# A transformer kernel of four blocks: the order of the first loads, the queue of the residual rows, the room of the returning probabilities and the place of a weight product

## The chip, the cores and the metric

The kernel runs on one core of a Trainium2 chip. The metric is the device time of one execution in microseconds (us), as the median of several runs. A core has five engines, each with its own instruction stream: TensorE (PE: matrix products and transposes through the array; PEld is its weight load), VectorE (DVE), ScalarE (ACT), GpSimd (POOL) and SyncE (SP). In this kernel nearly all DMA transfers are issued by SP, some by POOL. An engine works through its own stream in order: an instruction that waits holds everything behind it on the same engine, DMA issues included.

## The reference

x has the shape (2, 1024, 512): 2048 tokens, 16 tiles of 128. Four blocks with residuals; the second and the fourth are the same FFN:

```python
x = x + attn_a(layernorm(x), ...)   # chunked linear attention with decay
x = x + ffn(layernorm(x), ...)      # quantised codes: (w - 128) * scale
x = x + attn_b(layernorm(x), ...)   # softmax attention
x = x + ffn(layernorm(x), ...)      # the same weights again
```

```python
# attn_a, per chunk of 128 tokens and head of 128 (4 heads)
k     = k / max(norm(k), 1e-12)
cla   = cumsum(log(sigmoid(x Wa + ba) + 1e-6))
attn  = (q k^T) * beta * tril(exp(cla - cla^T))
y     = attn v + (q state) * exp(cla)
state = state * exp(cla_end) + v^T (k * beta * exp(cla_end - cla))
# ffn, hidden 1408
out = qlinear(silu(qlinear(x, gate)) * qlinear(x, up), down)
# attn_b, one head of 512, no mask
out = softmax(Q K^T / sqrt(512)) V Wo
```

Everything is float32.

## The kernel before

**Precision.** [...] `split` (L68) writes the high half with ScalarE and the difference with VectorE (or with GpSimd where `eng` says so). `mm3` (L82 to L87) then makes a product from three: high x high (L83), high x low (L84), low x high (L85). A product of 128x128 weights with 512 columns is one instruction of the "128x512" kind. `load_split` (L73) loads a block of 128x512 into a staging room (`stg`, four rooms) and splits it. `parts` collects the low halves' instructions, so that later code can be placed behind them.

**Order.** The program is traced, and a scheduler then sets the order of the instructions of each engine from its own estimate of times. `behind(list)` (L61) forces what is issued inside it to come after the instructions in the list; it is used as an order, not as a semaphore. Memory is given out by pools: a tile with a tag takes one of the tag's rooms and waits until the room's last reader is done.

**The opening** (L655 to L693). Warming matmuls, then M = Wq Wk^T (`weight_product`, L149; it is computed because attention B needs it; names pM, operands "M"), in four blocks over the inner dimension: each block is one lhs and one rhs of 128x512. Between the blocks come the layer norms of the first four token tiles (`ln_tile`, `layernorm_T`, L113): statistics on VectorE (L102, L104), the inverse root on GpSimd (`rs`, L108), the normalised tile `xn` (L110), four transposes in the array (`pxT`, L118), and the split of the result (`xh`, `xl`). Then the projections with Wk (pWk), Wq (pq) and Wv (pWv), for which each weight block is loaded and split. `spill` (L166) splits M and stores it to DRAM (`m_d`).

**Attention A** (loop L714 to L752) goes over the 16 token tiles. One iteration has the projections of a later tile, the scores (pS), the decay, the local part (pl, L640), the state's part (pg, L645), the state's update (pd, L606), and work of the next stages (`fill[t]`, `moving`). Decay needs a row of cumulated logs that returns through DRAM (`load_row`, row, L512 on GpSimd and L532 on SP). For the norm of k, ss (L572, L573, VectorE) gives s by a power on GpSimd (L575), and s times beta (L576) is used in `at` (L625), which pl reads. kw (L583, GpSimd) is what pd reads. In the last three iterations the second weight product, V = Wv Wo (pV, four blocks, `product_operands`, L140, used by attention B), and the first products of the FFN stand between the tiles. In the last-but-one iteration the order is: decay(15), then fill, down_weights, V's blocks 1 and 2, the last k norm (`late_norm`, behind those blocks' splits), the FFN's first weights, and three `moving` steps (`combine`, L229: differences `xT_f` of token halves and their splits B_f and T_f).

**FFN** (`ffn`, used twice as f and g): seven products of half matrices per hidden block (pX, pY, pZ, pV with weights wcf or wcg, L324), then the down projection (pof, pog, L870 and L871). Its gate and up weights are combined by GpSimd once (`stationary`, L297, lines L307 to L310), stored in DRAM and loaded back for later passes (L313).

**Attention B.** Scores of two 128-row tiles at a time stand in four PSUM banks (psX, psY, psZ, psV, L969). `softmax` (L1004): maximum on VectorE (L1007, L1009), exponential on ScalarE into a room tagged `pe` (L1014), sum and its inverse. `probs_T` (L1022) must turn the tile of probabilities so that the array can use it as weights: VectorE turns blocks of 32x32 (`py`, L1041), SP stores this to DRAM (`p_d`, L1045), and four loads bring it back in its new order (L1056). These land in the room of `ptl`, the low half, and are split there in place by `probs_split` (L1061: `pth` high, `ptl` low). Tile 14 alone is turned by TensorE (`ppt`, L1036). Tile 15 alone lands in a room tagged `pe` ("raw"). `out_b` (L1073) loads the residual rows (`xrb`, L1077), multiplies the probabilities with v (pob, 24 products per tile), adds (L1081) and stores the rows to x3 (L1082). The tags `pe`, `py`, `ptl`, `pth` have two rooms each; `xres`, where xrb stands, has three, so the load of tile t's rows waits until the rows of tile t-3 are stored. All of L1045, L1056, L1077 and L1082 are on SP's queue, in the scheduler's order.

**GpSimd in the span of attention B**: the inverse roots for the norms (`rs_b`, `rs_g`, L108) and some moves of turned tokens (`ln_move`, L188, DMA issue L196: `xT_b`, `xT_g`). Nothing of `xrb`.

Of the kernel before, what the change touches and what calls it, by code (L numbers as in the profile page):

```python
# [9 lines left out]
F32 = mybir.dt.float32  # L10
# [6 lines left out]
P = 128  # L17
D = 512
KD = D // P
T = 1024  # L20
NB = 2
NT = NB * T // P
# [3 lines left out]
ST = 4  # L26
# [8 lines left out]
def hybrid_block_kernel(ctx: ExitStack, tc: tile.TileContext, a, out):  # L35
# [34 lines left out]
        c = nc.scalar.copy(hi, src)  # L70
        return c.ins, (eng or nc.vector).tensor_tensor(lo, src, hi.bitcast(F32), ALU.subtract).ins  # L71

    def load_split(w, sp, src_ap, name, eng=None):  # L73

        stg = sp.tile([P, 512], F32, tag="stg", name=f"stg_{name}")
        load = nc.sync.dma_start(out=stg, in_=src_ap).ins
        cast, low = split(w[:, 0:512], w[:, 512:1024], stg, eng)
        parts.append(low)
        return cast, load
# [33 lines left out]
    def layernorm_T(xin, xT, i, name):  # L113

        xn = layernorm(xin, name)
        ps = psum(f"pxT_{name}").rearrange("p (k c) -> p k c", k=KD)
        for k in range(KD):
            nc.tensor.transpose(ps[:, k, :], xn[:, k * P : (k + 1) * P], ident)  # L118
        xh, xl = xT
        cs = bass.ts(i, P)  # L120
        split(xh[:, :, cs], xl[:, :, cs], ps)

    cols = cp.tile([P, H + 2 * KH], F32, name="cols")
    bq_s, sg_s, su_s = cols[:, 0:H], cols[:, H : H + KH], cols[:, H + KH : H + 2 * KH]
# [12 lines left out]
    m_d = [dp.tile([P, 1024], F32, tag=f"m_{k}", name=f"m_{k}") for k in range(KD)]  # L137


    def product_operands(sp, lhsT_d, rhs_d, name, k):  # L140

        w = slot(f"{name}{k}")
        lw, rw = w[:, 0:1024], w[:, 1024:2048]
        load_split(lw, sp, lhsT_d[k * P : (k + 1) * P, :], f"{name}l{k}")
        eng = nc.gpsimd if name == "M" else None
        cast, _ = load_split(rw, sp, rhs_d[k * P : (k + 1) * P, :], f"{name}r{k}", eng)
        return lw, rw, cast

    def weight_product(operands, name):  # L149
# [184 lines left out]
    with ExitStack() as actx:  # L334
# [41 lines left out]

        def load_wqkv(nm, staged=None):
            two = [slot(f"{nm}{n}") for n in range(2)]
            wqkv[nm] = [two[k // 2][:, k % 2 * 1024 : (k % 2 + 1) * 1024] for k in range(KD)]
            for k in range(KD):  # L380
                w, eng = wqkv[nm][k], nc.gpsimd if k % 2 else None
                if staged is None:
                    _, load = load_split(w, sp, a[nm][k * P : (k + 1) * P, :], f"{nm}{k}", eng)
                else:
                    split(w[:, 0:512], w[:, 512:1024], staged[:, k], eng)
            return load if staged is None else None

        xa = [x_in[t * P : (t + 1) * P, :] for t in range(NT)]

        def ln_tile(t):  # L390
            st, i = divmod(t, ST)
            if i == 0:
                xTa[st] = new_xT(f"a{st}")
            tag = "xres" if t < 8 and t % 4 > 1 else "xin"
            layernorm_T(xs[t] if t < 4 else load_x(xa[t], f"a{t}", tag), xTa[st], i, f"a{t}")

        def gate_proj(st):

# [258 lines left out]
            nc.tensor.matmul(pw[:, 0:P], ones, ones, start=i == 0, stop=i == WARM - 1)  # L657
        loads, xs = [], []
        prep = weight_product(loads, "M")
        loads.append(product_operands(sp, a["WqT"], a["WkT"], "M", 0))  # L660
        for k in range(KD):
            if k + 1 < KD:
                loads.append(product_operands(sp, a["WqT"], a["WkT"], "M", k + 1))
            if k < 2:
                xs += [load_x(xa[t], f"a{t}", "xres" if t > 1 else "xin") for t in (2 * k, 2 * k + 1)]
            if k == 2:

                staged = yp.tile([P, 4, KD, ST, 32], F32, tag="y", name="y_Wk")
                staged = staged.rearrange("p k a b c -> p k (a b c)")
                for m in range(KD):  # L670
                    nc.sync.dma_start(out=staged[:, m], in_=a["Wk"][m * P : (m + 1) * P, :])
                load_wab()
            pm, end = next(prep)
            with behind((end, loads[-1][2])):
                for t in ((), (0, 1), (2, 3), ())[k]:
                    ln_tile(t)
        load_consts()
        with behind((*normed_x, *parts[-2:])):
            load_wqkv("Wk", staged)
        with behind((end,)):  # L680
            kv_part(0, "Wk")
        wq_loaded = load_wqkv("Wq")
        spill(ap, ("kT", "kw", "sdec", "at"), pm, m_d, "M")
        for i in range(4):
            ends.clear()
            q_head(0, i)
# [27 lines left out]
        for t in range(NT):  # L714
            if t + 4 < NT:
                q_head(*divmod(t + 4, ST))
            if t == 0:
                decay_rows(0)
                load_row(0)
                load_row(1)  # L720
            load_row(t + 1)
            if (t + 2) % ST:
                load_row(t + 2)
            if t + 1 < NT:
                kv_tile(t + 1)
            weighed = scores(t)
            if t + 1 < NT:
                with behind((*normed[t + 1][2:], *key_copy)):
                    decay(t + 1)
            with behind(normed.get(t + 1, (weighed,))):  # L730
                for step in fill[t]:
                    step()
                if 1 <= t <= KH:
                    down_weights(sp, t - 1)
                for n in {NT - 3: (0,), NT - 2: (1, 2), NT - 1: (3,)}.get(t, ()):
                    loads.append(product_operands(sp, a["WvT"], a["Wo"], "V", n))
                if t == NT - 2:
# [161 lines left out]
    with ExitStack() as bctx:  # L899
# [122 lines left out]
        def probs_T(b, i):  # L1022


            t = b * NK + i
            pe, ri = pes[t]
            if t == NT - 2:

                lo = bp.tile([P, NK, P], F32R, tag="ptl", name=f"ptl{t}")
                hi = bp.tile([P, NK, P], F32R, tag="pth", name=f"pth{t}")  # L1030
                for s in range(2):
                    ps = psum(f"ppt{t}_{s}").rearrange("p (k c) -> p k c", k=4)
                    ks = slice(s * 4, s * 4 + 4)
# [11 lines left out]
            nc.sync.dma_start(  # L1045
                out=p_d[i].rearrange("k p f -> p k f"), in_=y.rearrange("p (k f) -> p k f", k=NK)
            )
            lo = bp.tile([P, NK, P], F32R, tag="ptl", name=f"ptl{t}")
            hi = bp.tile([P, NK, P], F32R, tag="pth", name=f"pth{t}")
            raw = lo.bitcast(F32)  # L1050
            if t == NT - 1:

                raw = bp.tile([P, T], F32, tag="pe", name=f"raw{t}").rearrange("p (k c) -> p k c", k=NK)
            placed = p_d[i].rearrange("k (c j) (r q) -> r j (k c) q", c=4, r=4)
            for r in range(4):
                nc.sync.dma_start(  # L1056
                    out=raw[32 * r : 32 * (r + 1)].rearrange("p k (c q) -> p (k c) q", c=4), in_=placed[r]
                )
            ptT[t] = hi, lo, raw, ri
# [13 lines left out]
        def out_b(b, i):  # L1073
            t = b * NK + i
            hi, lo, _, ri = ptT[t]
            xr = rp.tile([P, D], F32, tag="xres", name=f"xrb{t}")
            nc.sync.dma_start(out=xr, in_=x2[t])  # L1077
# [4 lines left out]
            nc.sync.dma_start(out=x3[t], in_=xr)  # L1082
            return end
# [189 lines left out]
```

## Time and profile before

| | us |
|---|---|
| median of 3 runs | 950.49 (950.21 to 950.91) |
| the profiled execution | 951.1 |
| its span in the trace | 949.4 |
| TensorE busy | 935.0 |
| VectorE busy | 725.2 |
| ScalarE busy | 412.0 |
| GpSimd busy | 219.1 |
| mean granted TensorE clock | 0.996 |

The profile is of one execution. A line of the timeline gives the start, the duration, the engine, the source line, the operation, what is written and what is read (by the program's names, buffer numbers left out), and in brackets how long the engine stood idle before it and what released it. "PE pl L640 <- DVE at L625: 2.2, 1, 2.2" in the list of waits says that the product pl waited for VectorE's `at`, 2.2 us in total, once, 2.2 us at the longest. In the windows, the number before "(x..)" is an engine's busy time in that stretch; then come the mean granted clock of TensorE, the DMA engines' share and GB/s.

By the chain of work that ended last, 86% of the span belongs to TensorE, 5% to VectorE and 3% to DMA:

```profile
PE 86%; DVE 5%; DMA 3%; SPq 2%; ACT 2%; issue 1%; POOL 1%; ACTq 0%; POOLq 0%; DVEq 0%
```

### The profile page before, as it was taken

The page shows a single profiled execution, that of the slowest core. Times are in us where ns is not written, and L with a number is a line of the kernel's source. Part 1 is how long each engine was busy: PE and PEld are TensorE (multiplying, and loading weights), DVE is VectorE, ACT ScalarE, POOL GpSimd, SP SyncE. Part 2 cuts the span into 40 slices and gives each one's busy share as a digit, 9 for nine tenths or more (in the row PEclk, how much of TensorE's full clock was granted, in tenths as well). Part 3 has the DMA queues.
Part 4 walks back from the last instruction along what each step waited for, and adds up shares of the span by engine and source line. Part 5 has one row for each costly group of instructions (what it writes and reads, how often), then busy time and mean ns, then how long its engine had stood idle before and what let it go on. Part 6 is the DMA issues. An engine that isn't in the chain of part 4 may idle for free.

```text
span 949.4 us, 13214 instructions
## 1 busy us (share of the span) xinstructions
PE 935.0 (98%) x4402; PEld 775.8 (82%) x4402; DVE 725.2 (76%) x1457; ACT 412.0 (43%) x795; POOL 219.1 (23%) x318
## 2 busy tenths in 40 slices
PE   8999999999999999999999999999989999999998
PEld 7788888887788888888888888888878888888887
DVE  7757767778899699787947877658868876976655
ACT  6554434336466434454324534235434443534421
POOL 5333323443355011120120400030400431001100
PEclk9999999999999999999999999999999999999999
DMA  9526456674898458742761989326989762573022
GB/s 322 178 90 175 137 133 167 186 193 161 292 363 267 106 199 298 183 84 78 264 146 45 173 167 212 135 36 132 190 166 312 276 169 45 189 243 137 37 65 81
DMA packets 215861, 162.18 MB, mean 171 GB/s; under 512 B 150960, under 2 KB 166640, under 8 KB 215792
## 3 DMA queue, kind: packets, MB, share of 16 engines
q1 hardware_dynamic: 213488, 156.61, 56.6%
q0 software_dynamic: 2304, 4.72, 3.3%
q8 instruction: 35, 0.57, 0.3%
q14 instruction: 34, 0.28, 0.1%
HBM read 104.76 MB, written 41.84 MB: 154 GB/s over the span
## 4 chain that ended last, share of the span: by engine, by line
PE 86%; DVE 5%; DMA 3%; SPq 2%; ACT 2%; issue 1%; POOL 1%; ACTq 0%; POOLq 0%; DVEq 0%
PE pXf L324 4%; PE pog L871 4%; PE pog L870 4%; PE pZf L324 4%; PE pVg L324 4%; PE pVf L324 4%; PE pZg L324 4%; PE pXg L324 4%; PE pof L871 3%; PE pof L870 3%; PE pob L85 3%; PE pob L83 3%; PE pob L84 3%; PE psV L969 2%; PE psZ L969 2%; PE psX L969 2%
## 5 line engine op out<-in xcount | busy, mean ns | idle before, releaser
L870 PE MATMUL pog<-wdg,hsg 128*128 128x512 f32 (+1 forms) x165 | 60.1, 375 | 0.0
L871 PE MATMUL pog<-wdg,hsg 128*128 128x512 f32 (+1 forms) x165 | 60.1, 375 | 0.0
L871 PE MATMUL pof<-wdf,hsf 128*128 128x512 f32 x154 | 59.3, 390 | 0.4 <-DVE ve_b L106 0.4
L870 PE MATMUL pof<-wdf,hsf 128*128 128x512 f32 x154 | 59.2, 390 | 0.0
L83 PE MATMUL pob<-vh,pth 128*128 128x512 f32 x128 | 50.8, 397 | 2.5 <-ACT pth L70 2.5
L85 PE MATMUL pob<-vh,ptl 128*128 128x512 f32 x128 | 50.8, 397 | 0.0
L84 PE MATMUL pob<-vl,pth 128*128 128x512 f32 x128 | 50.4, 394 | 0.0
L71 POOL TENSOR_TENSOR hsg<-sgg,hsg 128x128 fp32r<-128x128 f32 x40 | 17.9, 469 | 130.9 <-ACT hsg L70 130.9
L324 PE MATMUL pVf<-T_f,wcf 128*128 128x512 f32 x176 | 46.6, 389 | 0.0
L324 PE MATMUL pXg<-B_g,wcg 128*128 128x512 f32 x176 | 46.6, 389 | 0.0
L324 PE MATMUL pXf<-B_f,wcf 128*128 128x512 f32 x176 | 46.5, 394 | 0.0
L324 PE MATMUL pVg<-T_g,wcg 128*128 128x512 f32 x176 | 46.3, 389 | 0.0
L108 POOL TENSOR_TENSOR rs_b<-ve_b,mhalf 128x1 f32<-128x1 f32 x16 | 11.6, 728 | 141.6 <-DVE ve_b L106 137.4
L108 POOL TENSOR_TENSOR rs_g<-ve_g,mhalf 128x1 f32<-128x1 f32 x16 | 9.6, 604 | 137.9 <-DVE ve_g L106 137.9
L196 POOL DMA_DIRECT2D xT_g<-y_g x48 | 30.9, 652 | 40.5 <-DVE T_b L71 29.0
L324 PEld LDWEIGHTS pXf<-B_f,wcf 128*128 128x128 f32 x176 | 33.3, 190 | 7.1 <-DMA wcf<-wc 0.3
L324 PEld LDWEIGHTS pVf<-T_f,wcf 128*128 128x128 f32 x176 | 33.1, 188 | 6.9
L324 PEld LDWEIGHTS pVg<-T_g,wcg 128*128 128x128 f32 x176 | 33.1, 188 | 6.9
L324 PEld LDWEIGHTS pXg<-B_g,wcg 128*128 128x128 f32 x176 | 33.0, 188 | 6.9
L870 PEld LDWEIGHTS pog<-wdg,hsg 128*128 128x128 f32 x165 | 31.1, 188 | 5.7
L871 PEld LDWEIGHTS pog<-wdg,hsg 128*128 128x128 f32 x165 | 31.0, 188 | 5.6
L871 PEld LDWEIGHTS pof<-wdf,hsf 128*128 128x128 f32 x154 | 28.9, 188 | 6.8 <-DVE hsf L71 0.8
(335 smaller groups left out, 2737.9 us busy)
## 6 DMA issues: line engine op xcount, KB each, us to landing
wcg<-wc SPq DMA_DIRECT2D x22, 896.0 KB, 5.8
wc<-wcf SPq DMA_DIRECT2D x11, 896.0 KB, 5.3
wcf<-wc SPq DMA_DIRECT2D x11, 896.0 KB, 5.6
p<-py SPq DMA_DIRECT2D x15, 512.0 KB, 4.0
ptl<-p SPq DMA_DIRECT2D x56, 128.0 KB, 4.0
xin_a<-in_x SPq DMA_DIRECT2D x16, 256.0 KB, 4.5
xra<-in_x SPq DMA_DIRECT2D x16, 256.0 KB, 2.7
row<-cl SPq DMA_DIRECT2D x16, 256.0 KB, 3.7
```

Source lines behind the costliest of these rows:

```text
L71: return c.ins, (eng or nc.vector).tensor_tensor(lo, src, hi.bitcast(F32), ALU.subtract).ins
L83: nc.tensor.matmul(ps, lhs_hi, rhs_hi, start=first, stop=False)
L84: nc.tensor.matmul(ps, lhs_hi, rhs_lo, start=False, stop=False)
L85: end = nc.tensor.matmul(ps, lhs_lo, rhs_hi, start=False, stop=last).ins
L108: nc.gpsimd.tensor_tensor(rs, ve, mhalf, ALU.pow)
L196: (nc.sync if sync else nc.gpsimd).dma_start(out=xf[32 * b : 32 * (b + 1), :, c, :], in_=y[32 * c : 32 * (c + 1), b].rearrange("p k i q -> ...
L324: nc.tensor.matmul(ps, w[:, m, k * P : (k + 1) * P], o[:, s, k, :], start=first and k == 0 and s == 0, stop=k == 1 and s == 1, skip_group_ ...
L870: nc.tensor.matmul(ps, hs[i][0][:, j], wd[j][:, ds], start=j == 0, stop=False)
L871: nc.tensor.matmul(ps, hs[i][1][:, j], wd[j][:, ds], start=False, stop=j == KH - 1)
L969: ends[nm] = nc.tensor.matmul(ps, o[:, i, k], w[:, j, k], start=first and k == 0 and i + j == 0, stop=k == 1 and i == 1, skip_group_check= ...
```

## The change

1. **Opening loads.** All eight blocks of M are loaded first. The blocks 2 and 3 go to a room tagged `y` that is free at that time, instead of waiting for `stg` rooms. Then come the four token tiles, Wab, Wk (now in the `stg` rooms), the constants, and Wq (now staged in the `y` room). pM's blocks are ordered among the token tiles: tiles 0 and 1 behind block 2, tiles 2 and 3 behind block 3. M's spill is placed behind Wq's splits. `layernorm_T` returns its last transpose for this.
2. **Rows of the decay.** `load_row(t + 2)` is written at the end of an iteration instead of its beginning. `decay(t + 1)` for the tiles 7 and 15, which have no `normed[t + 1][2:]`, is placed behind that of the tile before.
3. **V.** V's blocks 1 and 2, and the k norm of the last tile, are issued before the rest of the last-but-one iteration, behind `key_copy` alone.
4. **Probabilities.** The four loads of every tile (not of tile 15 alone) land in a room tagged `pe`, which the exponentials use too. The split reads it there and writes `pth` and `ptl`.
5. **Residual rows.** xrb's 16 loads are issued by GpSimd's queue instead of SP's.

In the order that is built, the engines' streams differ so: in the opening TensorE runs blocks 0 to 2 of pM, the transposes of tiles 0 and 1, block 3, the transposes of tiles 2 and 3, pWk, and so on; GpSimd makes M's low halves 2 and 3 before the first `rs_a`. At V, VectorE's splits of blocks 1 and 2 stand before xT_f's first difference, `ss` and s x beta of tile 15 directly behind V's splits, and `at` of tile 15 before two T_f splits; GpSimd's s of tile 15 stands behind four of the weight sums instead of six; row 15 stands behind kw of tile 14. In attention B, ScalarE's `pth` casts of tiles 3, 5 and 7 stand before or nearer to the exponentials of later tiles, and 16 products of FFN g stand after the second of the 24 products of pob15. The xrb loads stand between `rs_b`, `rs_g` and the xT_g moves on GpSimd.

```diff
-    def load_split(w, sp, src_ap, name, eng=None):
-
-        stg = sp.tile([P, 512], F32, tag="stg", name=f"stg_{name}")
+    def load_split(w, sp, src_ap, name, eng=None, stg=None):
+
+        if stg is None:
+            stg = sp.tile([P, 512], F32, tag="stg", name=f"stg_{name}")
...
-    def product_operands(sp, lhsT_d, rhs_d, name, k):
+    def product_operands(sp, lhsT_d, rhs_d, name, k, rooms=(None, None)):
...
-        load_split(lw, sp, lhsT_d[k * P : (k + 1) * P, :], f"{name}l{k}")
+        load_split(lw, sp, lhsT_d[k * P : (k + 1) * P, :], f"{name}l{k}", None, rooms[0])
...
-        loads.append(product_operands(sp, a["WqT"], a["WkT"], "M", 0))
+        room = staging("M")
         for k in range(KD):
-            if k + 1 < KD:
-                loads.append(product_operands(sp, a["WqT"], a["WkT"], "M", k + 1))
-            if k < 2:
-                xs += [load_x(xa[t], f"a{t}", "xres" if t > 1 else "xin") for t in (2 * k, 2 * k + 1)]
...
-            pm, end = next(prep)
-            with behind((end, loads[-1][2])):
-                for t in ((), (0, 1), (2, 3), ())[k]:
-                    ln_tile(t)
+            rooms = (room[:, 2 * k - 4], room[:, 2 * k - 3]) if k > 1 else (None, None)
+            loads.append(product_operands(sp, a["WqT"], a["WkT"], "M", k, rooms))
+        xs += [load_x(xa[t], f"a{t}", "xres" if t > 1 else "xin") for t in range(ST)]
+        load_wab()
+        split_M = parts[-2:]
+        turned = []
+        for k in range(KD):
+            with behind(turned):
+                pm, end = next(prep)
+            with behind((end,)):
+                turned = [ln_tile(t) for t in ((), (), (0, 1), (2, 3))[k]]
+        with behind((*normed_x, *split_M)):
+            load_wqkv("Wk")
         load_consts()
-        with behind((*normed_x, *parts[-2:])):
-            load_wqkv("Wk", staged)
+        staged = staging("Wq")
+        for m in range(KD):
+            wq_loaded = nc.sync.dma_start(out=staged[:, m], in_=a["Wq"][m * P : (m + 1) * P, :]).ins
         with behind((end,)):
             kv_part(0, "Wk")
-        wq_loaded = load_wqkv("Wq")
-        spill(ap, ("kT", "kw", "sdec", "at"), pm, m_d, "M")
+        with behind(load_wqkv("Wq", staged)):
+            spill(ap, ("kT", "kw", "sdec", "at"), pm, m_d, "M")
...
-            if (t + 2) % ST:
-                load_row(t + 2)
...
-                with behind((*normed[t + 1][2:], *key_copy)):
+                with behind((*(normed[t + 1][2:] or normed[t][2:]), *key_copy)):
                     decay(t + 1)
+            if t == NT - 2:
+                with behind(key_copy):
+                    for n in (1, 2):
+                        loads.append(product_operands(sp, a["WvT"], a["Wo"], "V", n))
+                with behind(parts[-4:]):
+                    late_norm.pop()()
...
-                for n in {NT - 3: (0,), NT - 2: (1, 2), NT - 1: (3,)}.get(t, ()):
+                for n in {NT - 3: (0,), NT - 1: (3,)}.get(t, ()):
                     loads.append(product_operands(sp, a["WvT"], a["Wo"], "V", n))
-                if t == NT - 2:
-                    with behind(parts[-4:]):
-                        late_norm.pop()()
...
+            if (t + 2) % ST:
+                load_row(t + 2)
...
-            raw = lo.bitcast(F32)
-            if t == NT - 1:
-
-                raw = bp.tile([P, T], F32, tag="pe", name=f"raw{t}").rearrange("p (k c) -> p k c", k=NK)
+
+            raw = bp.tile([P, T], F32, tag="pe", name=f"raw{t}").rearrange("p (k c) -> p k c", k=NK)
...
-            nc.sync.dma_start(out=xr, in_=x2[t])
+            nc.gpsimd.dma_start(out=xr, in_=x2[t])
```

More of the change, by code (lines that the diff above doesn't have):

```diff
@@ L117, in layernorm_T @@
         for k in range(KD):
-            nc.tensor.transpose(ps[:, k, :], xn[:, k * P : (k + 1) * P], ident)
+            turned = nc.tensor.transpose(ps[:, k, :], xn[:, k * P : (k + 1) * P], ident).ins
         xh, xl = xT
@@ L121, in layernorm_T @@
         split(xh[:, :, cs], xl[:, :, cs], ps)
+        return turned
     cols = cp.tile([P, H + 2 * KH], F32, name="cols")
@@ L137, in hybrid_block_kernel @@
     m_d = [dp.tile([P, 1024], F32, tag=f"m_{k}", name=f"m_{k}") for k in range(KD)]
-    def product_operands(sp, lhsT_d, rhs_d, name, k):
+    def product_operands(sp, lhsT_d, rhs_d, name, k, rooms=(None, None)):
         w = slot(f"{name}{k}")
         lw, rw = w[:, 0:1024], w[:, 1024:2048]
-        load_split(lw, sp, lhsT_d[k * P : (k + 1) * P, :], f"{name}l{k}")
+        load_split(lw, sp, lhsT_d[k * P : (k + 1) * P, :], f"{name}l{k}", None, rooms[0])
         eng = nc.gpsimd if name == "M" else None
-        cast, _ = load_split(rw, sp, rhs_d[k * P : (k + 1) * P, :], f"{name}r{k}", eng)
+        cast, _ = load_split(rw, sp, rhs_d[k * P : (k + 1) * P, :], f"{name}r{k}", eng, rooms[1])
         return lw, rw, cast
@@ L378, in load_wqkv @@
             two = [slot(f"{nm}{n}") for n in range(2)]
+            done = []
             wqkv[nm] = [two[k // 2][:, k % 2 * 1024 : (k % 2 + 1) * 1024] for k in range(KD)]
@@ L384, in load_wqkv @@
                 else:
-                    split(w[:, 0:512], w[:, 512:1024], staged[:, k], eng)
-            return load if staged is None else None
+                    done.extend(split(w[:, 0:512], w[:, 512:1024], staged[:, k], eng))
+            return load if staged is None else done
         xa = [x_in[t * P : (t + 1) * P, :] for t in range(NT)]
@@ L394, in ln_tile @@
             tag = "xres" if t < 8 and t % 4 > 1 else "xin"
-            layernorm_T(xs[t] if t < 4 else load_x(xa[t], f"a{t}", tag), xTa[st], i, f"a{t}")
+            return layernorm_T(xs[t] if t < 4 else load_x(xa[t], f"a{t}", tag), xTa[st], i, f"a{t}")
         def gate_proj(st):
@@ L659, in hybrid_block_kernel, with staging @@
         prep = weight_product(loads, "M")
-        loads.append(product_operands(sp, a["WqT"], a["WkT"], "M", 0))
+        def staging(name):
+            y = yp.tile([P, 4, KD, ST, 32], F32, tag="y", name=f"y_{name}")
+            return y.rearrange("p k a b c -> p k (a b c)")
+        room = staging("M")
         for k in range(KD):
-            if k + 1 < KD:
-                loads.append(product_operands(sp, a["WqT"], a["WkT"], "M", k + 1))
-            if k < 2:
-                xs += [load_x(xa[t], f"a{t}", "xres" if t > 1 else "xin") for t in (2 * k, 2 * k + 1)]
[L666 to L672, printed above, removed]
-            pm, end = next(prep)
-            with behind((end, loads[-1][2])):
-                for t in ((), (0, 1), (2, 3), ())[k]:
-                    ln_tile(t)
+            rooms = (room[:, 2 * k - 4], room[:, 2 * k - 3]) if k > 1 else (None, None)
[11 more added lines that the diff above has]
+            load_wqkv("Wk")
         load_consts()
-        with behind((*normed_x, *parts[-2:])):
-            load_wqkv("Wk", staged)
+        staged = staging("Wq")
+        for m in range(KD):
+            wq_loaded = nc.sync.dma_start(out=staged[:, m], in_=a["Wq"][m * P : (m + 1) * P, :]).ins
         with behind((end,)):
             kv_part(0, "Wk")
-        wq_loaded = load_wqkv("Wq")
-        spill(ap, ("kT", "kw", "sdec", "at"), pm, m_d, "M")
+        with behind(load_wqkv("Wq", staged)):
+            spill(ap, ("kT", "kw", "sdec", "at"), pm, m_d, "M")
         for i in range(4):
```

## The prediction

> **What bounds the kernel now.** I read the totals first, then TensorE's list of waits, then windows and timelines around the long waits. The totals:
>
> ```profile
> PE 935.0 (98%) x4402; PEld 775.8 (82%) x4402; DVE 725.2 (76%) x1457; ACT 412.0 (43%) x795; POOL 219.1 (23%) x318
> ```
>
> TensorE is busy 935.0 of 949.4 us, and the change takes no matrix product away. So a gain can only come out of 949.4 - 935.0 = 14.4 us of idle time and out of time at a low clock. TensorE's waits (us in total, times, longest):
>
> ```profile
> PE pob L83 <- ACT pth L70: 2.5, 1, 2.5
> PE pl L640 <- DVE at L625: 2.2, 1, 2.2
> ...
> PE pxT_a L118 <- DVE xn_a L110: 1.0, 3, 0.4
> PE pV L84 <- DVE V L71: 1.0, 1, 1.0
> ...
> PE pd L606 <- POOL kw L583: 0.5, 1, 0.5
> ```
>
> All five stand where the change works: the opening (pxT_a), the product V (pl, pV, pd) and the last tiles of attention B (pob). The windows (PE, PEld, DVE, ACT, POOL busy, then the clock) show that two waits cost more than themselves:
>
> ```profile
> 230.00:240.00 10.00, 8.48 (x48) 7.11 (x48) 9.19 (x21) 6.07 (x9) 6.45 (x8) 1.00 0.78 284
> 240.00:250.00 10.00, 9.19 (x42) 8.07 (x43) 7.85 (x17) 3.86 (x7) 4.61 (x6) 0.83 0.76 285
> ...
> 690.00:700.00 10.00, 8.11 (x36) 6.28 (x34) 4.97 (x9) 0.43 (x2) 0.00 (x0) 1.00 1.16 214
> 700.00:710.00 10.00, 9.42 (x37) 7.44 (x38) 7.70 (x14) 7.27 (x16) 0.00 (x0) 0.83 0.60 122
> ```
>
> After each of the two longest waits the clock is 0.83 for 10 us, and matmuls run at 0.63 instead of 0.39:
>
> ```profile
> 700.58 0.50 PE L83 MATMUL pob<-vh,pth 128*128 128x512 f32 x1 [2.47 <-ACT pth L70]
> ...
> 704.36 0.62 PE L83 MATMUL pob<-vh,pth 128*128 128x512 f32 x1
> 704.79 0.43 PE L84 MATMUL pob<-vl,pth 128*128 128x512 f32 x1
> 705.06 0.39 PE L85 MATMUL pob<-vh,ptl 128*128 128x512 f32 x1
> ```
>
> 0.17 of 10 us is 1.7 us lost after each. Gaps of 0.4 to 1.0 us elsewhere lie in windows with clock 1.00.
>
> [...] Here 2.22 and 2.47 us were enough. [...]
>
> **The change part by part.**
>
> *Opening loads.* No work is taken out; eight blocks of M are issued back to back. Before, blocks 5 to 8 waited for staging rooms and were issued at 4.79, 6.31, 6.86 and 8.01. An issue takes 0.42 to 0.47, so the eighth now leaves near 0.81 + 7 x 0.47 = 4.1. pM started at 4.97 and pWk at 20.06: 15.09 us for 48 products x 0.2275 + 16 transposes x 0.11 = 12.7, so 2.4 are lost there. All three early pxT_a waits (1.0), M's wait (0.2) and the slow first matmul after each switch make these up. In the new order only two switches between pM and transposes remain (0.55), so pWk begins some 1.9 sooner. Behind it VectorE is the limit (9.61 and 9.94 of 10 us busy from 10 to 30), and every row of it stays. The tokens' loads stand behind M's: nine blocks of 256 KB at the window's 272 to 359 GB/s are 6.6 to 8.7 us, so the first tile lands near 9 (an estimate), where its statistics began at 7.11. GpSimd also makes M2's and M3's low halves (1.29 to 1.38 each) ahead of the four rs_a. So xn_a0 comes near 11, as before (11.01), and xn_a3 near 14; pM's blocks cover them until 13.7 and 17.3. Without that cover, what they are late comes straight off the gain. Bounds: 0.5 (VectorE keeps its old end, only late idle time goes) to 2.8 (2.4 and the 0.46 before pxT_a7). I take 1.8, since the VectorE order has the token tiles ahead of M's spill.
>
> *V sooner, decay of tiles 7 and 15 later.* (The moved `load_row(t+2)` leaves SP's order as it was: nothing.) Three waits stand in a row: 0.53 before pd (GpSimd's row select waits 3.67 for its load at 217.43 and kw14 stands behind it), 1.02 before pV, 2.22 before pl. The last chain is
>
> ```profile
> 234.66 2.35 DVE L71 TENSOR_TENSOR T_f<-xT_f,T_f 128x1024 fp32r<-128x1024 f32 x2
> 236.93 0.16 DVE L573 TENSOR_SCALAR ss<-ss 128x4 f32<-128x4 f32 x1
> ...
> 239.62 0.68 DVE L576 TENSOR_TENSOR s<-s,beta 128x4 f32<-128x4 f32 x1 [0.70 <-POOL s L575]
> 240.40 1.13 DVE L625 SCALAR_TENSOR_TENSOR at<-pS,s,dec 128x128 f32<-128x128 f32 x4
> ```
>
> The new order puts ss and its partners ahead of the two T_f splits (2.35), so `at` comes at least 2.35 sooner and the 2.22 closes. GpSimd's s15 then stands behind four weight sums instead of six. kw14 goes ahead of row15, which closes the 0.53; V's splits ahead of xT_f's difference (1.21) close the 1.02. With 1.7 of clock: 0.53 + 1.02 + 2.22 + 1.7 = 5.5. What is late next: VectorE, 9.4 to 10.0 of 10 us busy from 250 on; the splits pushed back land there. It gains its own idle time (2.79 before 219.07, 0.70, 2.01 before 245.33), which is more than it gives, so most stays. Bounds: 5.5, and 2.2 where FFN f returns 2 and one gap stays at 1.3 without the clock loss. I take 5.0 and 0.7 returned: 4.3.
>
> *Residual rows on GpSimd's queue.* SP loses 16 issues of 0.32 to 0.34, and above all their place: there, an xrb load waits until an earlier store has landed, and all behind it wait too:
>
> ```profile
> 684.81 0.32 SPq L1082 DMA_DIRECT2D x<-xrb  x1
> 688.92 0.32 SPq L1077 DMA_DIRECT2D xrb<-x  x1
> 689.33 1.23 SPq L1045 DMA_DIRECT2D p<-py  x2
> 693.72 5.93 SPq L1056 DMA_DIRECT2D ptl<-p  x8
> ```
>
> py12 was ready at 686.89, so its write goes 2.4 sooner. GpSimd gains 16 DMA issues; its nearest row is 0.652 each (xT_g, x48): 10.4 us on an engine with 23% busy. Queued behind them are rs_g and xT_g moves. By the before trace these start at 581.87, 598.71, 631.73, 668.94, 678.15 and 731.81, all after the store that the load ahead of them needs. I cost it at nothing; without that cover a late rs_g only delays FFN g's inputs, which are used after 725. SP waits 24.1 us at L1077 in ten places; only at tile 12 does TensorE wait at its end, so only that one is counted.
>
> The landing times are 3.4 to 3.7 us on GpSimd's queue (xT_b, xT_g) and 3.1 on SP's (xrb), and a row is loaded one tile or more (5.5 us of pob) ahead of its use, so the later landing is covered.
>
> [...]
>
> *Probabilities into the exponentials' room.* The loads no longer wait for `ptl`. But there are two such rooms, so the exponentials of tile t+2 now wait for tile t's low split. On ACT pth3 is ahead of exp4, pth5 ahead of exp6. Before, ptl2's split ended at 552.4 and exp4 began at 552.6, so tile 4 just fits; exp5 (its split ended 559.4, its load landed about 554) comes 2 to 3 us later. TensorE has scores and out_b in hand then, so I put zero, upper bound in rival three. At the end: pth12 came at 699.91 and comes near 697.5 to 698.3, TensorE is ready at 698.1: 2.47 + 1.7 = 4.1 to gain. Then exp14 and exp15 wait for the splits of tiles 12 and 13: pth12 697.7, ptl12 and the maxima to 700.3, exp14 to 701.7, ptl13 703.7, exp15 705.1, py15 about 705.2, and 11.2 later as before (706.22 to 717.42) pth15 at 716.4. TensorE, 4.1 earlier than 719.81, wants it at 715.7, and the first weights of FFN g (issued behind raw15's loads, near 713.4, 5.8 to land) at 719.2. So 1 to 3 us of new waiting. Bounds -0.2 to 4.1, taken: 1.5.
>
> **Sum** on the profiled 951.1 (span 949.4 + 1.7): 951.1 - 1.8 - 4.3 - 1.5 = 943.5. That run is 0.6 above the median 950.49, so 942.9.
>
> **The rivals.**
> *One: the last stage gives all back.* pob15 and FFN g's first weights wait over 2.2 us, with a second clock loss. For it: the ring above. Against: FFN g products were put between. Tail 0: 950.5 - 6.1 = 944.4.
> *Two: VectorE takes the opening and V back.* For: it is full at 10 to 30 and 250 to 310. Opening 0.5, V 2.2, tail 1.5: 950.5 - 4.2 = 946.3.
> *Three, slower: two rooms are too few.* Exponential, transpose, write, load, split, next exponential become one ring. From exp12 (684.10) to ptl13's end (705.10) it took 21.0, or 19 without SP's 2 us; pairs follow each other every 17 to 23 us (exponentials at 684.1 and 701.0). Where TensorE runs out, 2.2 + 1.7 = 3.9 each; six such links stand inside the two batches, and it decides from three on: 950.5 - 6.1 + 11.7 = 956.1. Against: pob waits only once in 16 tiles now, and the loads start sooner.
> *Four: all gains in full*, 2.8 + 5.5 + 4.1 = 12.4: 938.1.
> *Five: the change doesn't do what it says.* The built order shows each move, so only through some other wait: within 0.2%.
>
> **How the numbers follow.** Forecast 0.50, one 0.17, two 0.10, four 0.08: faster. Three 0.10: slower. Five 0.05. A difference under 0.2% (1.9 us) can't be told from none. Faster 0.85, same 0.05, slower 0.10. The range 938.1 (rival four) to 948.0 (the low bounds, 950.5 - 0.5 - 2.2 + 0.2) leaves out rival three and most of five; the likeliest case alone is 940.5 to 945.
>
> **What would show it.** Right: pq before 23.2; no wait over 0.5 us on pd, pV and pl, clock 1.00 from 230 to 250; the first load of tile 12 by 691.5 and no clock loss at pob12; a wait of 1 to 3 us before pob15 or FFN g's first product. Wrong: waits on pob or on scores at several pairs behind pth (rival three), rs_g or xT_g late behind L1086, VectorE idle-free with TensorE waiting on B_f or T_f splits in FFN f.

## The result, and the profile after

| | before | after |
|---|---|---|
| median, 6 runs each, same chip | 951.35 us (950.21 to 952.61) | 958.81 us (958.63 to 960.1) |
| ratio, 95% interval | | 1.0081 (1.0068 to 1.0094) |
| the profiled execution | 951.1 | 959.36 |
| its span | 949.4 | 957.6 |
| mean granted TensorE clock | 0.996 | 0.995 |

The change makes the kernel 7.5 us slower, where 942.9 was forecast. The totals and the shares of the chain on the page after:

```profile
PE 937.2 (98%) x4402; PEld 776.1 (81%) x4402; DVE 724.8 (76%) x1457; ACT 411.4 (43%) x795; POOL 235.4 (25%) x334
...
PE 84%; DVE 6%; DMA 5%; SPq 3%; ACT 1%; issue 1%; POOL 0%; ACTq 0%; DVEq 0%
```

The work is the same (4402 matmuls), so the 8.2 us by which the span grew are idle time and slow clock; the chain of waits now leans on DMA (5%, it was 3%) and SP's issues (3%, it was 2%). TensorE's waits after (us in total, times, longest):

```profile
PE pob L84 <- ACT pth L70: 5.2, 2, 4.3
PE pXg L326 <- DMA wcg<-wc: 3.4, 1, 3.4
PE pxT_a L119 <- DVE xn_a L111: 1.3, 2, 0.9
...
PE pVf L326 <- ACT hbf L811: 1.0, 1, 1.0
PE pz L418 <- DVE ab L410: 0.8, 1, 0.8
...
PE pof L881 <- ACT hsf L70: 0.7, 1, 0.7
PE pab L406 <- DVE xl_a L71: 0.6, 1, 0.6
```

The three waits of V (pl 2.2, pV 1.0, pd 0.5) are gone. In their place stand waits in the opening (pab, pz, pxT_a), a longer wait for the probabilities of tile 12, and a new one for FFN g's first weights. The windows of after (PE, PEld, DVE, ACT, POOL busy, clock, DMA share, GB/s):

```profile
230.00:240.00 10.00, 10.00 (x63) 8.83 (x63) 8.73 (x19) 5.42 (x8) 3.92 (x4) 1.00 0.85 286
240.00:250.00 10.00, 10.00 (x48) 8.36 (x47) 9.96 (x21) 6.09 (x11) 6.43 (x8) 1.00 0.54 192
...
690.00:700.00 10.00, 6.71 (x30) 5.12 (x28) 2.04 (x4) 0.00 (x0) 0.00 (x0) 0.97 0.83 170
700.00:710.00 10.00, 9.01 (x33) 7.33 (x34) 6.36 (x14) 6.38 (x14) 0.54 (x1) 0.69 0.53 91
...
720.00:730.00 10.00, 5.68 (x18) 3.93 (x17) 4.10 (x5) 1.75 (x3) 0.00 (x0) 0.84 0.93 330
```

At V, TensorE is full at full clock: the gain came. At 700 to 710 the clock is 0.69 (0.83 before), and at 720 to 730, where before had a full window at 1.00, TensorE works 5.68 of 10 us. To see where along the program the time went, I compared the start of the same matmul in each profile with before's (us; negative is sooner; worked out from the timelines; two profiles of one code differ by up to 1; the rows below the first are of runs told of further down):

```
                        pWk   pd of    first   attention B's  tile 12  tile 15   end
                        first tile 14  pY of f  first scores   pob      pob
after                  -1.68   0.88    -4.66      -1.54        0.41     2.09    8.17
V alone                -0.33  -0.83    -6.36      -2.67       -2.22    -2.17   -2.16
opening alone          -0.62   4.61     3.22       3.75        3.86     3.89    3.90
rows alone              0.42   0.96     1.70       1.86        2.58     2.47    7.63
rooms alone            -0.38   0.86     0.10       2.20        1.46     0.59    6.87
after, order kept      -0.60   2.07    -3.48      -0.70        0.67     0.77    1.24
end turned alone        0.21   0.66     1.02       0.88        1.21     1.41    3.65
tokens sooner          -0.45  -0.26    -0.59       0.06       -0.26    -1.87   -1.64
V and tokens sooner    -0.27  -1.17    -6.72      -3.06       -3.03    -3.09   -3.08
```

After: pWk begins 1.7 sooner, but by V the kernel is 0.9 late; V brings 5.5, FFN f takes 3.1 back; from attention B's first scores to the end 9.7 are lost, 6.1 of them behind tile 15's first product.

### The profile page after: what moved, and what is told of

Read it like the earlier page. It is cut to its first block, busy times and chain, and to the rows that moved or that the text cites. A ratio compares the mean times of both kernels' runs of the same rounds, so it can differ in the third digit from the quotient of the medians.

```text
span 957.6 us, 13198 instructions
## 1 busy us (share of the span) xinstructions
PE 937.2 (98%) x4402; PEld 776.1 (81%) x4402; DVE 724.8 (76%) x1457; ACT 411.4 (43%) x795; POOL 235.4 (25%) x334
## 4 chain that ended last, share of the span: by engine, by line
PE 84%; DVE 6%; DMA 5%; SPq 3%; ACT 1%; issue 1%; POOL 0%; ACTq 0%; DVEq 0%
PE pog L882 4%; PE pog L881 4%; PE pVg L326 4%; PE pZg L326 4%; PE pXg L326 4%; PE pVf L326 4%; PE pof L882 4%; PE pof L881 4%; PE pXf L326 4%; PE pZf L326 4%; PE pob L86 2%; PE pob L84 2%; PE pob L85 2%; PE pYg L326 2%; PE pYf L326 2%; PE psV L980 2%
## 5 line engine op out<-in xcount | busy, mean ns | idle before, releaser
L70 ACT CAST pth<-raw 128x512 fp32r<-128x512 f32 x30 | 17.1, 618 | 49.5 <-DMA raw<-p 49.4
L1086 POOL DMA_DIRECT2D xrb<-x x16 | 9.2, 573 | 109.4 <-DMA x<-xrb 62.4
```

The lines of the kernel that those rows point to most:

```text
L1086: nc.gpsimd.dma_start(out=xr, in_=x2[t])
```

## The experiments

Each time is a median; each ratio, with its 95% interval, is to the kernel before measured alongside it. The numbers 1 to 5 below name the change's parts: opening (1), V's place (2) with `load_row`'s (3), the room of the returning probabilities (4), the residual rows' queue (5).

**One part undone.** Rows back on SP's queue in the kernel after; and, in another, the rooms as before:

```diff
-            nc.gpsimd.dma_start(out=xr, in_=x2[t])
+            nc.sync.dma_start(out=xr, in_=x2[t])
```

> The changed kernel with the 16 residual-row loads back on SP's queue, all else as changed (958.8 us). Theory A (the rows' transfers on GpSimd's queue run beside the writes of the probabilities and slow them: p of tile 12 took 6.33 us from issue to landing, where 4.0 was usual): the write lands in 4 to 4.5 us, the wait before pob12 falls from 4.3 to under 1.5 us, the time falls by 4 us or more, to 955 or less. Theory B (the shared rooms make a ring of exponential, transpose, write, loads, split; the queue matters little): the wait stays over 3 us and the time within 2 us of 958.8.

```diff
-            raw = bp.tile([P, T], F32, tag="pe", name=f"raw{t}").rearrange("p (k c) -> p k c", k=NK)
+            raw = lo.bitcast(F32)
+            if t == NT - 1:
+                raw = bp.tile([P, T], F32, tag="pe", name=f"raw{t}").rearrange("p (k c) -> p k c", k=NK)
```

> The changed kernel with the probabilities landing in ptl again (tile 15 alone in the exponentials' room), all else as changed. Theory B: the exponentials of tiles 14 and 15 no longer wait for the splits of 12 and 13, py15 is written 2 us sooner or more after pth12, the waits before pob15 (0.9) and for FFN g's first weights (3.4) go with the low clock behind them, some 6 us: about 952.5. Theory A: these waits follow from the late landing of tile 12; the wait before pob12 stays near 4.3 and the time within 2 us of 958.8.

Rows on SP: 956.81, ratio 1.0060 (1.0040 to 1.0079); tile 12's wait falls from 4.28 to 1.33, the wait for wcg is 3.62 (3.40 in after). Rooms as before: 954.39, 1.0036 (1.0026 to 1.0046); tile 12 still waits 3.79, wcg 1.03. So the rows make tile 12 late, and the rooms have a hand in the wait for wcg. Neither accounts for all of it. The DMA issues of 684 to 700 us (size, median us from issue to landing), after:

```profile
p<-py SPq DMA_DIRECT2D x2, 512.0 KB, 8.5
...
xrb<-x POOLq DMA_DIRECT2D x2, 256.0 KB, 8.7
```

and with the rows on SP's queue:

```profile
p<-py SPq DMA_DIRECT2D x2, 512.0 KB, 5.2
...
xrb<-x SPq DMA_DIRECT2D x1, 256.0 KB, 3.0
```

The rows' move slows both transfers, the row's own (3.0 to 8.7) and SP's write of the probabilities (5.2 to 8.5). It is not the queue by itself: over all 16 rows of after the median to landing is 3.4, and the row issued at 704.64 took 2.97. The chain of waits of after (start, us, engine) shows SP's loads of tile 12 slowed too:

```profile
684.89 6.33 DMA p<-py
...
691.67 2.28 SPq L1065
694.00 2.73 SPq L1065
696.77 3.45 DMA raw<-p
...
711.22 3.22 DMA p<-py
...
715.55 1.96 SPq L1065
...
718.87 7.12 DMA wcg<-wc
```

One issue of a 128 KB load takes SP 2.28 and 2.73 us here while rows are on their way on the other queue; these are the second and third of tile 12's four. With the rows on SP's queue the same two took 0.64 and 0.94, before 0.62 and 0.71. Tile 12's write left at 684.89, 4.4 sooner than before (689.33), and its probabilities are cast at 700.3, 0.4 later than before. Part of the write's slowness is not the rows': at 684.89 the moves of xT_g, which are on GpSimd's queue in before too, are still under way, and with the rows on SP's queue a write that left at 686.87 beside these moves took 5.84 (the run at the end of this section), against 4.34 in before.

**One part alone**, on the kernel before: V with `load_row` (2, 3), and the opening (1), each as the change's own lines.

> The kernel before with the two changes around V alone (V's splits and the last norm sooner, rows of the decay later). By the traces the changed kernel went from 0.9 us behind at pd of tile 14 to 1.4 us ahead in the middle of attention B: a gain of 2.3 to 3.0, 948.5 us. Rival (FFN f's full VectorE takes the gain back whole): 951 us, within 0.7 of before.

> The kernel before with the new opening alone. Theory C (the tokens land 3 us later, VectorE starts its full stretch later and ends it later): 1.4 to 1.9 us slower, 953 us, with TensorE waiting on VectorE at pab, pz, pxT of tiles 4 and 7 (2.8 us together). Rival, as predicted: 1.8 us faster, 949.5 us.

V alone: 948.14, 0.9961 (0.9947 to 0.9975); run again, on another chip, 948.38, 0.9946 (0.9934 to 0.9959):

> V alone once more: 948.1 as in e3, 3 us under before, pl and pd without a wait over 0.5 us and no half clock from 230 to 250 us.

The windows of V alone show what closing three waits gives:

```profile
230.00:240.00 10.00, 10.00 (x66) 8.96 (x65) 8.70 (x19) 6.09 (x9) 4.00 (x4) 1.00 0.76 271
240.00:250.00 10.00, 10.00 (x46) 8.28 (x45) 10.00 (x21) 6.75 (x11) 4.71 (x7) 1.00 0.63 243
```

The opening alone: 954.48, 1.0028 (1.0015 to 1.0041), slower by 2.7. TensorE's waits in after's opening (timeline; in brackets the idle time before, and its releaser):

```profile
22.91 0.44 PE L406 MATMUL pab<-xl_a,wab 128*48 128x512 f32 x1 [0.62 <-DVE xl_a L71]
...
30.83 0.60 PE L418 MATMUL pz<-fold,ab 48*128 48x8 f32 x4 [0.83 <-DVE ab L410]
...
32.29 0.66 PE L119 MATMUL pxT_a<-ident,xn_a 128*128 128x128 f32 x4 [0.86 <-DVE xn_a L111]
...
39.82 0.66 PE L119 MATMUL pxT_a<-ident,xn_a 128*128 128x128 f32 x4 [0.46 <-DVE xn_a L111]
```

All four name VectorE, at 23 to 40 us. In the opening alone there are four as well (0.79, 0.68, 0.80 and 0.85), and the last two, at 31 to 33 us, are followed by half clock: 0.50 from 33.51 to 36.93 (0.83 on average from 30 to 40). VectorE's first statistics began at 7.11 before; in after:

```profile
10.19 1.27 DVE L103 BATCH_NORM_STATS2 bn_a<-xin_a 128x6 f32<-128x512 f32 x2
```

The tokens stand behind all of M in the new order of loads. If that is the cause, moving the token loads ahead of M's last four blocks should undo it:

```diff
+            if k == 2:
+                xs += [load_x(xa[t], f"a{t}", "xres" if t > 1 else "xin") for t in range(ST)]
             loads.append(product_operands(sp, a["WqT"], a["WkT"], "M", k, rooms))
-        xs += [load_x(xa[t], f"a{t}", "xres" if t > 1 else "xin") for t in range(ST)]
```

> The new opening alone (e4, 954.5) with the four token loads issued ahead of M's last four blocks. Theory C (VectorE idles until the tokens land and is full afterwards, so what they are late comes out at the end of the opening): the first statistics begin at 7 to 8.5 us instead of 10.2 to 11.3, pxT of tile 7 comes 2 us or more sooner, 951.5 to 952.5. Rival (the order of M's spill, Wq and the decay's inputs behind it): pz and pxT of tile 4 still wait 0.8 each, the time stays within 1 us of 954.5.

> The changes around V with the opening of e13. Theory C: as V alone or better, 947 to 948.5. Rival: 950 or more.

On the opening alone this gives 949.59 against 953.62, 0.9963 (0.9950 to 0.9976), and the four waits are gone (one of 0.58, for GpSimd's low half of M, has come at 13 us). Its first statistics:

```profile
7.46 1.34 DVE L103 BATCH_NORM_STATS2 bn_a<-xin_a 128x6 f32<-128x512 f32 x2
```

So the place of the token loads decides. But the way from there to the waits is not the one that I had expected, an idle VectorE that never catches up. While the tokens were on their way VectorE split M's blocks, which in before came later; and at 20.15 in before and 20.33 in after it has the same work behind it (four splits of M and two of Wk, four sets of statistics, four xn, two xl). And with the tokens sooner it comes to its first split of Wk at 18.02, in the opening alone at 18.05: the earlier statistics have gained it nothing by then. There the two part. The rows of VectorE and GpSimd, each splitting two of Wk's four blocks, in the opening alone:

```profile
17.78 3.00 POOL L71 TENSOR_TENSOR Wk<-stg_Wk,Wk 128x512 fp32r<-128x512 f32 x2 [1.43 <-ACT Wk L70]
18.05 3.28 DVE L71 TENSOR_TENSOR Wk<-stg_Wk,Wk 128x512 fp32r<-128x512 f32 x2
```

and with the tokens sooner:

```profile
18.02 4.14 POOL L71 TENSOR_TENSOR Wk<-stg_Wk,Wk 128x512 fp32r<-128x512 f32 x2 [2.61 <-ACT Wk L70]
18.02 1.28 DVE L71 TENSOR_TENSOR Wk<-stg_Wk,Wk 128x512 fp32r<-128x512 f32 x2
```

Where GpSimd's first began 0.27 us ahead, VectorE's two took 3.28; where both began at 18.02, VectorE's two took 1.28, and GpSimd's 4.14 instead of 3.00. One after the other, VectorE's four splits of Wk and Wq take 1.58, 1.78, 1.45 and 1.16 us in the opening alone, and 0.68, 0.69, 1.47 and 0.68 with the tokens sooner. That is 2.5 less, and `ab`, which pz waits for, comes 2.2 sooner (28.98 for 31.14). After has slow ones too (1.67, 1.78, 1.40 and 1.16), with GpSimd's 0.17 ahead; why GpSimd starts 0.27 ahead in the one and level in the other was not looked into.

With V it is 948.03, 0.9942 (0.9929 to 0.9954), faster than both kernels; V alone, measured alongside, has 0.9946, so the two gains do not add by anything that can be told. The kernel before took 953.62 in these last runs, 2 us more than in the others, and by its single profile the tokens sooner gain 0.9 up to the first pWv and 1.6 in all; the 0.9963 may be too good.

**The end.** In before, all 24 products of tile 15 stand in one block ahead of FFN g. In after, 2 of them come, then 16 products of FFN g, which wait for wcg, then the other 22. I held FFN g's first products behind the last of tile 15, on the kernel after:

```diff
-                    for ps, n in ((X, "P1"), (Y, "P6"), (Z, "P5"), (V, "P7")):
-                        products(ps, w, nm, pr, n, True)
+                    with behind(held if pr == 0 and j == 0 else ()):
+                        for ps, n in ((X, "P1"), (Y, "P6"), (Z, "P5"), (V, "P7")):
+                            products(ps, w, nm, pr, n, True)
```

> The changed kernel with FFN g's first 16 products held behind pob15 (the changed order put them after its second product, where their weights have not landed). Theory D (that place costs 3.4 us of waiting and the half clock behind it): the wait on wcg and the clock loss after it go, pob15 runs in one piece, 4 to 6 us faster: 953 to 955. Rival (the weights are late whatever runs first, the wait only moves): within 1.5 us of 958.8.

A miss: 957.64, 1.0054 (1.0038 to 1.0069). The wait for wcg is gone, but tile 15 then waits itself, 0.45 for its high and 1.40 for its low half. The rows and the rooms, each alone on the kernel before:

> The kernel before with the residual rows on GpSimd's queue alone. Theory A: the loads of tile 12 are slowed as in the changed kernel (SP's issues of 2 us and more while two rows are in flight on the other queue), pob12 waits 3.5 to 4.5 us, and the built order again puts 16 products of FFN g into pob15: 955 to 958. Rival, as predicted (SP's place is free, p of tile 12 leaves 2.4 us sooner): 948 to 949.

> The kernel before with the probabilities landing in the exponentials' room alone, rows on SP. Theory B and D: pob12 waits no longer than before (2.5), but exponentials 14 and 15 come after the splits of 12 and 13, and FFN g's products stand in pob15: 2 to 5 us slower, 953.5 to 956. Rival, as predicted: the new wait eats what pob12 gains, 951, within 1 us of before.

Rows alone: 956.13, 1.0044 (1.0022 to 1.0066). Rooms alone: 958.33, 1.0067 (1.0048 to 1.0086). Either makes the end late, and the table above shows it: 5 to 6 us behind tile 15's start. ScalarE's timeline at the end of after, where before has `pth` (717.42) ahead of T_g (718.47):

```profile
717.65 2.00 ACT L70 CAST T_g<-xT_g 128x1024 fp32r<-128x1024 f32 x2 [5.98 <-DVE xT_g L246]
719.56 1.04 ACT L70 CAST B_g<-xT_g 128x1024 fp32r<-128x1024 f32 x1
721.23 1.14 ACT L70 CAST pth<-raw 128x512 fp32r<-128x512 f32 x2 [0.62 <-DMA raw<-p]
```

So the scheduler had turned the order round: FFN g's casts first, tile 15's behind them, and TensorE's products to match. It does so with the rows alone and with the rooms alone; it does not with V or the opening alone. Nothing in the diff names these instructions. To price it, I put that order into the kernel before, with nothing else changed:

```diff
-        probs_split(1, 7, last)
         with behind(splits):
             do(moving, 6)
+        probs_split(1, 7, [turned_last[0]])
```

> The kernel before with one order alone taken from the changed kernel: tile 15's casts stand behind the casts of T2, T3 and B21 of the next FFN, and with that 16 products of FFN g stand after the second of pob15. Theory E (this order of the end is most of the loss; the rooms and the queue only made the planner choose it): TensorE waits 2.5 us or more for wcg, the half clock follows, 4 to 7 us slower, 955.5 to 958.5. Rival (the loss comes from the rooms or the queue themselves): within 1 us of before.

(`turned_last` holds the cast of the last B_g.) The turned order alone costs 956.17, 1.0042 (1.0024 to 1.0060), about 4 us by the medians. Its profile shows less of it: the wait for wcg is 1.17, not the 2.5 or more that I had expected, no half clock follows, and 2.2 are lost behind tile 15's start. And the other way: before's order forced by hand, with the rooms alone, the rows alone, and the whole change:

```diff
-        probs_split(1, 7, last)
+        casts = probs_split(1, 7, last)
         with behind(splits):
-            do(moving, 6)
+            do(moving, 3)
+        with behind(casts):
+            do(moving, 3)
```

(and FFN g held as above)

> The kernel before with the probabilities in the exponentials' room (alone it took 958.3), and the end's order of before kept by hand: T2, T3, B21 behind tile 15's casts, FFN g's first products behind pob15. Theory E: the 6 us fall away, 950 to 952.5. Theory B (the ring of two rooms costs by itself): 954 or more, with waits before pob12 and pob15 over 2 us.

> The kernel before with the residual rows on GpSimd's queue (alone it took 956.1), and the end's order of before kept by hand. Theory A and E together: the wait on wcg goes, the slow issues of tile 12's loads stay, pob12 waits 3 us or more: 952 to 954. Rival (all of the queue's loss was the order): 951 or less, and the second and third load of tile 12 are issued in under 1 us.

> The changed kernel with the end's order of before kept by hand (both orders). Theory E: 4 us or more under the changed kernel's 958.8. By the single parts: 951.4 + 2.7 (opening) - 3.2 (V) + 2 (rows) + 0 to 1 (rooms) = 953 to 954. Rival (the parts' losses are in the rooms and the queue): 956.5 or more.

Rooms: 953.47, 1.0011 (0.9994 to 1.0028), no difference that can be told, though in its one profile, the slowest of its ten executions (956.62), tile 12 waited 4.01. Rows: 954.19, 1.0021 (1.0003 to 1.0038). The whole change: 954.45, 1.0030 (1.0016 to 1.0044), against 1.0081 without this order. By the ratios the order kept gives back 5.3, 2.2 and 4.9 us. TensorE's waits at the end of the last one, from its timeline:

```profile
701.25 0.76 PE L84 MATMUL pob<-vh,pth 128*128 128x512 f32 x1 [3.82 <-ACT pth L70]
...
720.58 0.50 PE L84 MATMUL pob<-vh,pth 128*128 128x512 f32 x1 [0.19 <-ACT pth L70]
```

and ScalarE's:

```profile
719.91 1.14 ACT L70 CAST pth<-raw 128x512 fp32r<-128x512 f32 x2 [8.82 <-DMA raw<-p]
720.95 2.00 ACT L70 CAST T_g<-xT_g 128x1024 fp32r<-128x1024 f32 x2
722.85 1.04 ACT L70 CAST B_g<-xT_g 128x1024 fp32r<-128x1024 f32 x1
```

Tile 15's cast is ahead of T_g again. The wait for wcg is gone and the one at tile 15 is 0.19; tile 12's stays, as the rows are still on GpSimd's queue.

**A version to beat both, which did not.** V, with tile 13's rows forced behind the writes of tiles 12 and 13 on SP's queue, and FFN g held:

> The kernel before with the changes around V, and two orders by hand: residual row 13 (on SP) behind the writes of p of the tiles 12 and 13, and FFN g's first products behind pob15. Theory A/D: the write of p12 no longer waits 2 us behind row 13's load, GpSimd's queue has only the moves, so pob12's wait falls from 3.0 to 1.3 or less and no half clock follows: 3 us under V alone, 945. Rival (p12's earlier write only meets the moves of xT_g in flight, and lands no sooner): the time of V alone, 948.

951.91, 0.9999 (0.9987 to 1.0012): V's gain was lost again. The write of tile 12 left 1.26 us after its turn began, but landed 5.8 later; and the scheduler put tile 15's casts behind FFN g's (tile 15 waited 1.82 and 1.65).

## Why the prediction was wrong

Added up from the runs that measure each part by itself (the ratio's excess over 1, times 951): opening +2.7, V -3.7 to -5.1, rooms with the order that they bring +6.4, rows with the order kept +2.0. That is 6.0 to 7.4, and 7.5 was measured. With the order kept the parts give 0.6 to 2.0 (the rooms 1.0), and 2.9 was measured, with intervals of 1 to 2 us on each. The prediction had -1.8 for the opening, -4.3 for V, nothing for the rows and -1.5 for the end.

**Opening: the step that failed is "Behind it VectorE is the limit (9.61 and 9.94 of 10 us busy from 10 to 30), and every row of it stays".** pWk did begin 1.7 sooner, and pq at 21.9 (the prediction's mark was 23.2); 1.8 was taken from that. But VectorE's rows did not stay. In after its four splits of Wk and Wq take 6.0 us beside GpSimd's, 4.9 before; and a fourth set of statistics and `ss` now stand ahead of `ab`, which comes at 30.09 instead of 28.31. xn of tile 4 comes at 31.69 instead of 30.34. So VectorE's end moved later, which the low bound ("VectorE keeps its old end") had ruled out, and the delay came out as TensorE's waits of 0.62, 0.83, 0.86 and 0.46. xn_a0, forecast near 11, came at 13.08, without a wait at TensorE in after and with 0.79 in the opening alone. That run also lost 1.7 to half clock, after waits that by the prediction's reading ("gaps of 0.4 to 1.0 us") cost nothing more. The prediction's count of the early pxT_a waits, 1.0, has 0.16 in it that lies behind pWk's start (at 30.94).

**V: right.** All three waits closed, the clock is 1.00 from 230 to 250 as the prediction named it, and the gross gain of 5.5 is what the timelines give (0.88 to -4.66). The mis-sized part is what FFN f returns: 0.7 was taken, 3.1 came (-4.66 to -1.54), 2.6 of it as waits before pVf (1.0), pof (0.7), pYf (0.5) and pXf (0.4), where before had 0.4. By the ratios the two runs of V alone kept 3.7 and 5.1, by their single profiles 2.2 and 1.4; the profiled executions were 0.9 and 1.5 above the medians, which covers part of it, and the rest is open.

**Rows on GpSimd's queue: the step that failed is "I cost it at nothing".** The write went 4.4 sooner (1.5 of this because the whole kernel was ahead), and the first load of tile 12 left at 691.29, by the prediction's mark of 691.5. It bought nothing, because the write and the loads behind it ran beside the xT_g moves and the rows on the other queue: SP took 9.48 us to issue the eight loads, 5.93 before. "The landing times are 3.4 to 3.7 us" held for the rows in the median (3.4), but these two took 8.3 and 9.0. The prediction asked whether the row itself, and GpSimd, could afford the move, and they could; it did not ask what a second queue in flight does to the first. By the runs that cost +2.0 with the order kept. What they show is slower neighbours on both queues; why the two rows themselves took 8.3 and 9.0 is not shown.

**Rooms: the term "2.47 + 1.7 = 4.1 to gain" never came, and rival three's place was wrong.** No ring of two rooms formed: TensorE's pob waits twice in all, at tiles 12 and 15, and at no pair before. By themselves, with the order kept, the rooms cost nothing that can be told (1.0011, 0.9994 to 1.0028).

**The end: the step that failed is "FFN g products were put between", counted as cover.** The prediction saw the turned order and priced 1 to 3 us of new waiting by when weights and probabilities would land. What lay between were products whose weights were not there: SP issued them at 718.87 behind tile 15's loads (715.73 before), they landed near 726, and 22 products of tile 15 stood behind the ones that wait for them; in before, tile 15's whole block keeps TensorE busy until 725.25, so that wcg is not needed sooner. The waits before tile 15 and FFN g are 0.92 and 3.40, and the half clock after the second, 3.41 us from 726.78, costs 1.7 more. The turned order by itself is worth some 4 us (2.2 to 5.3 by the runs and the profile above), more than any other loss of the sum, and it was in no part of the diff.

Rival three had the sign and not the mechanism. With 0.10 on slower, the chances were set by gains each of which was argued at its own place; a part that only moves transfers had been allowed no way to lose.

**Open.** How the scheduler comes to turn the end round was not looked into. How rows and rooms share tile 12's loss is known only to about 1.5 us (the interval with the rooms alone and the order kept is 0.9994 to 1.0028). Rows on ScalarE's queue, which might give SP's relief without the other queue's price, were not tried. Tile 12's wait is 2.81 with the rows alone and 4.77 with the order kept, 1.58 and 4.01 with the rooms: its single profiles do not settle the shares.

## What to carry to other kernels

When loads are put in another order, work out anew the order and the lengths of the rows on every engine that they feed, not only on the one at the end of the chain: VectorE's splits took up to 1.78 us instead of 0.68 where GpSimd's had begun first, and came back as waits on TensorE at 23 to 40 us. Before moving transfers to a second queue, look at what is on the first queue at that time, since both were slowed here (the write of the probabilities from 5.2 to 8.5 us to landing, the row from 3.0 to 8.7). And where a scheduler sets the order, compare the whole order before and after, also where the edit doesn't reach; one turned pair of blocks cost more than any edited line, and two lines that pin the order brought the whole change from 1.0081 to 1.0030.

## What the runs showed of the hardware

**Two queues with traffic at once.** From 691 us of after, GpSimd's queue and SP's both carry traffic; KB per us, summed from the trace's packets:

```
                         SP's queue             GpSimd's queue
after,  4 us from 691    115   69  116   94     143  209  115   70
before, 3 us from 691    359  347  347            0    0    0
```

In these stretches SP's queue moved 69 to 116 KB per us in after and 347 to 359 in before; the two together moved 164 to 278 in after. (Before, it is the writes of the probabilities alone; from 691.3 on, after has tile 12's loads among SP's, and such loads by themselves moved 139 to 181 KB per us in before, from 694 on.) The eight 128 KB loads of the tiles 12 and 13 took SP 8.73 to 10.36 us to issue in five profiles with the rows on GpSimd's queue (after 9.48, rooms apart 10.36, FFN g held 9.51, rows alone 8.73, order kept 9.47), and 5.77 to 6.78 in six with the rows on SP's (before 5.93, rows back on SP 6.16, V alone 5.77, rooms alone 6.05, V and order 6.78, rooms with the order kept 5.95).

**Splits on VectorE and GpSimd at the same time.** In after a split of 128x512 with none under way on the other engine took VectorE 0.69 us (from 4.21) and GpSimd 1.28 (from 4.93). Later there GpSimd's ran from 16.79 to 18.09, and VectorE's, begun at 16.96, ended at 18.63; GpSimd's next, begun at 18.04, ended at 19.78, and VectorE's next, begun at 18.55, at 20.33. The three that began while the other engine's was under way took 1.67, 1.74 and 1.78. With the tokens sooner both engines began at 18.02: VectorE's two took 0.68 and 0.69, and GpSimd's two 4.14 together.

**Half clock beside waits.** In before the granted clock was 0.50 from 240.63 and from 701.43, for 3.41 us each, beside the waits of 2.22 (238.59 to 240.81) and 2.47 (698.11 to 700.58); beside the others behind the first 7 us, of 1.02 at the longest, it was 1.00. In after it was 0.50 for 6.83 us from 699.47, beside the wait of 4.28 (696.71 to 700.99), and for 3.41 from 726.78, behind those of 0.92 and 3.40 (the second ends at 726.03); beside its others behind the first 7 us, of 0.98 at the longest, it was 1.00. The length of one wait does not tell it in the other profiles: in the opening alone 0.80 and 0.85 us, 1.5 us apart, were followed by half clock, and 2.3 before pl were not (1.00 from 230 to 260). Before pl the rows alone and the rooms alone each waited 3.0, and from 240 to 250 the clock was 0.83 in the first and 1.00 in the second. What decides is not shown. 3.41 us at 0.50 are 1.7 us of TensorE's work, an estimate from these two numbers.
